# A graph layer's keys: products two tiles ahead, squares one tile ahead, and a count two steps later

## Chip, cores and metric

One core of a Trainium2 chip. The metric is the device time of one execution in microseconds (us). Engines are named as in the profile: PE (TensorE matmuls), PEld (its weight loads), DVE (VectorE), ACT (ScalarE), POOL (GpSimd), SP (SyncE).

## The reference, cut

There are 12500 nodes of 256 channels and 200000 edges, sorted by target. All is 32-bit.

```
xn = layernorm(x)                                   # no gain, no bias
gnn = relu(segment_sum((xn @ W)[src] * edge_weight, dst))
k, v = layernorm of each head of xn @ wk.T, xn @ wv.T   # 4 heads of 64, gain and bias
kv  = einsum('shd,she->hde', k, v) / 12500
mix = (q . kv, heads joined) @ wo.T + bo            # q = xn @ wq.T
x   = x + gnn + mix
h   = layernorm(x) * ln_w + ln_b
30 times: h = h + 0.01 tanh(h);  h = h sigmoid(h);  h = layernorm(h) @ W2 + b
out = x + h
```

## The kernel before, in words

The nodes are 98 tiles of 128 rows (TensorE's partitions), in 25 groups of four. The kernel runs in three parts.

**Part one, the norm (lines 580 to 619).** Step g = 0 to 26 loads a group of x, takes its statistics, shifts and scales it on ACT (line 521), transposes it (PE line 533 into a PSUM pool called p_t, copied by ACT line 539 to `xnT`, in the profile `big`), and works off the lists of edges. From g = 3 each step also takes one tile of *keys*, a class `KeyValue`: two matrix products, four matmul records, into a tile `pkv` of the PSUM pool p_kv, which has three buffers (line 290); the Square of it on ACT (line 297); the sums of squares per head on DVE (line 301); the square root on ACT (line 303); and, in `normed`, the reciprocal (line 307) and the product of `pkv` with it, `kn` (line 308), which is the last reader of the PSUM tile. There are three `kn` tiles, used in turn; the small tiles of this chain are in a pool of two buffers each. `kv_product(t)` sums the outer products of keys and values over all tiles in one PSUM tile `pacc` (PE line 316); it is called for the tile two before. So 24 tiles of keys are done in part one.

In step g = 22 (`NL` is 21) the function `any_outside` counts, on DVE, the edges whose target lies outside a fixed window of nodes; a matmul with a column of ones sums the count over partitions (line 557), and DVE turns it into a flag (line 558). After the loop all engines read the flag (line 621) and branch on it (line 626). The branch holds a slow way of summing edges; with these inputs it isn't entered, and the trace has no row of its lines.

**Part two, the loop over the remaining keys (lines 824 to 843).** It goes over tiles t = 24 to 97 and two steps more. Between the keys it sums edges. An indirect DMA on POOL (line 187, "gather") fetches the rows of `xn` of 128 edges to an SBUF tile `xg`, of which there are 16; eight gathers are an *octet*. `selections` builds on DVE the matrices that place the edges (lines 213, 218, 226: five operations for an octet). `sum_quad`, called twice for an octet, multiplies eight gathered tiles with them on PE (line 239, 16 records into `pq`); `copy_quads` copies `pq` on ACT in the step after (line 250); `add_quads` adds it to the ring of nodes `pa` on PE (line 261); `free_nodes` takes finished nodes from the ring (ACT line 275, DVE memset line 276). An octet's work is done in the steps that a small planner marks in `octet_at` (lines 802 to 808): t = 30, 33, 37, 41, 44, 48, 51, 55, 58, 62, 65, 69, 72, 76, 79, 83, 86 and 98. Two octets' gathers are issued ahead of the loop (line 809, `gathers(ROWS)`); the others follow the octet that frees their tiles, on POOL behind that octet's `pq`.

Within a step each engine has its instructions in the order of the code, for instance PE: product of t, `pacc` of t - 2, `pa`, `pq`. ACT: copy of `pq`, copy of the ring, Square of t, root of t. DVE: memset of the ring, sum of t, selections, small weights' work on some steps (`rest`), reciprocal and `kn` of t.

**Part three (from about 400 us to the end).** 30 rounds of the second network over all tiles, with the rest of the edges between them, in an order planned ahead on the host. It also uses p_kv in its first steps (lines 858 on).

Of the kernel before, what the change touches and what calls it, by code (L numbers as in the profile page):

```python
# [8 lines left out]
F32 = mybir.dt.float32  # L9
# [7 lines left out]
P = 128  # L17
# [14 lines left out]
def gps_layer(  # L32
# [22 lines left out]
    nc = tc.nc  # L55
    N, C = x.shape
# [3 lines left out]
    NT = -(-N // P)  # L60
# [7 lines left out]
    p_t = ctx.enter_context(tc.tile_pool(name="p_t", bufs=2, space=PSUM))  # L68
# [253 lines left out]
    kv_done = 0  # L322
    with ExitStack() as ph:
# [159 lines left out]
        nc.vector.tensor_scalar(w0p, tcol, jt, float(STEP // O), ALU.subtract, ALU.mult)  # L483
        nc.vector.tensor_scalar(w0p, w0p, float(OFF), 0.0, ALU.add, ALU.max)
        nc.vector.tensor_scalar(w0p, w0p, float(NT * P - WIN2), None, ALU.min)
        dfirst, dmin, dmax = (prep.tile([P, NCH], F32, name=n) for n in ("dfirst", "dmin", "dmax"))
        nc.vector.memset(dfirst, 0.0)
        nc.vector.memset(dmin, 1e9)
# [52 lines left out]
        def any_outside():  # L541

            lo = small.tile([P, NCH], F32, name="lo")
            nc.vector.tensor_tensor(lo, dfirst, w0p, ALU.max)
            hi = small.tile([P, NCH], F32, name="hi")
            nc.vector.tensor_scalar(w0p, w0p, float(WIN2), None, ALU.add)
            nc.vector.scalar_tensor_tensor(hi, dfirst, float(WIN), w0p, op0=ALU.add, op1=ALU.min)
            nc.vector.tensor_tensor(lo, dmin, lo, ALU.is_lt)
            nc.vector.tensor_tensor(hi, dmax, hi, ALU.is_ge)
            nc.vector.tensor_tensor(lo, lo, hi, ALU.add)  # L550
            cnt1 = small.tile([P, 1], F32, name="cnt1")
            nc.vector.tensor_reduce(cnt1, lo, AX.X, ALU.add)
            ones = prep.tile([P, 1], F32, name="ones")
            nc.vector.memset(ones, 1.0)
            flag_i = prep.tile([1, 1], I32, name="flag_i")
            pcnt = p_t.tile([1, 1], F32, name="pt")
            nc.tensor.matmul(pcnt, lhsT=cnt1, rhs=ones, start=True, stop=True)
            nc.vector.tensor_scalar(flag_i, pcnt, 1.0, None, ALU.min)
            return flag_i
# [20 lines left out]
        for g in range(NG + 2):  # L580
            if g + 2 < NG:
                load_x(g + 2)
            if g + 2 < NL:
                load_list(g + 2)
            if g >= 2:
                norm_of_x(g - 2)
            if 1 <= g <= NG:
                shift_of_x(g - 1)
            if g < NL:
                list_values(g)  # L590
            if 0 < g < NG:
                stats_of_x(g)
            if g == 1:
                nc.vector.tensor_reduce(hm, wh, AX.X, ALU.add)
                nc.vector.tensor_scalar(hm, hm, 1.0 / D, None, ALU.mult)
                nc.vector.tensor_tensor(wh, wh, hm[:, :, None].to_broadcast([P, KC * 2 * HEADS, D]), ALU.subtract)
            if 0 <= g - 2 < NL:
                list_stored(g - 2)
            kv = None
            if g >= 3:  # L600
                kv = KeyValue(kv_done)
                kv_done += 1
                kv.squares()
            if g >= 2:
                transposes_of_x(g - 2)
                copy_of_x(g - 2, 0)
            if kv:
                kv.deviations()
            if g >= 2:
                copy_of_x(g - 2, 1)  # L610
            if kv_done >= 3:
                kv_product(kv_done - 3)
            if 0 <= g - 1 < NL:
                list_extremes(g - 1)
                list_transposes(g - 1)
            if kv:
                kv.normed()
            if g == NL + 1:
                flag_i = any_outside()

        n_out = nc.values_load(flag_i[0:1, 0:1], min_val=0, max_val=1)


# [2 lines left out]
    with tc.If(n_out > 0):  # L626
        with ExitStack() as pg_:
# [12 lines left out]
            for t in range(NE):  # L640
                rows = P if t < EC else ER
                xg = gp.tile([P, C], F32, name="xg")
                nc.gpsimd.indirect_dma_start(
                    out=xg[:rows], out_offset=None, in_=xnd,
                    in_offset=bass.IndirectOffsetOnAxis(ap=src_i[:rows, t : t + 1], axis=0),
                )
                d_i = gp.tile([P, 1], I32, name="d_i")
                nc.sync.dma_start(out=d_i[:rows], in_=dst[t * P : t * P + rows].rearrange("(p o) -> p o", o=1))
                d = gp.tile([P, 1], F32, name="d")
                nc.vector.tensor_copy(d[:rows], d_i[:rows])  # L650
                d = d[:rows]

                w0 = float(win(t // O))
                o1 = gp.tile([P, 1], F32, name="o1")
                o2 = gp.tile([P, 1], F32, name="o2")
                ewl = gp.tile([P, 1], F32, name="ewl")
                r1 = rel[:rows, t : t + 1]
                nc.vector.tensor_scalar(o1[:rows], r1, 0.0, None, ALU.is_lt)
                nc.vector.scalar_tensor_tensor(
                    o2[:rows], r1, float(WIN) - 0.5, o1[:rows], op0=ALU.is_gt, op1=ALU.add  # L660
                )
                nc.vector.scalar_tensor_tensor(o1[:rows], d, w0 - 0.5, o2[:rows], op0=ALU.is_lt, op1=ALU.add)
                nc.vector.scalar_tensor_tensor(
                    o2[:rows], d, w0 + float(WIN2) - 0.5, o1[:rows], op0=ALU.is_gt, op1=ALU.add
                )
                nc.vector.scalar_tensor_tensor(
                    ewl[:rows], o2[:rows], 0.5, ew[:rows, t : t + 1], op0=ALU.is_gt, op1=ALU.mult
                )
                pb = p_t.tile([P, P], F32, name="pt")
                nc.tensor.transpose(pb[:, :rows], d.to_broadcast([rows, P]), ident[:rows, :rows])  # L670
                junk = gp.tile([P, P], F32, name="junk")
                cnt = gp.tile([P, 1], F32, name="cnt")
                nc.vector.scalar_tensor_tensor(
                    junk[:rows, :rows], pb[:rows, :rows], d, below[:rows, :rows], op0=ALU.is_equal,
                    op1=ALU.mult, accum_out=cnt[:rows],
                )
                sel = gp.tile([P, P], F32, name="sel")
                nc.vector.tensor_scalar(
                    sel[:rows, :rows], pb[:rows, :rows], d, ewl[:rows], ALU.is_equal, ALU.mult
                )  # L680

                move = gp.tile([P, 1], F32, name="move")
                nc.vector.tensor_sub(move[:rows], rowno[:rows], d)
                nc.vector.scalar_tensor_tensor(
                    move[:rows], cnt[:rows], 0.5, move[:rows], op0=ALU.is_gt, op1=ALU.mult
                )
                idx = gp.tile([P, 1], I32, name="idx")
                nc.vector.tensor_tensor(idx[:rows], move[:rows], d, ALU.add)
                pg = p_kv.tile([P, C], F32, name="pkv")
                nc.tensor.matmul(pg[:rows], lhsT=sel[:rows, :rows], rhs=xg[:rows], start=True, stop=True)  # L690
                ms = gp.tile([P, C], F32, name="ms")
                nc.scalar.copy(ms[:rows], pg[:rows])
                nc.gpsimd.indirect_dma_start(
                    out=acc, out_offset=bass.IndirectOffsetOnAxis(ap=idx[:rows, 0:1], axis=0),
                    in_=ms[:rows], in_offset=None, compute_op=ALU.add,
                )
            nc.sync.dma_start(out=wg, in_=gnn_weight.rearrange("(k p) c -> p k c", p=P))
            for gi, (t0, nt) in enumerate(groups):
                ac = gp.tile([P, G, C], F32, name="ac", bufs=1)
                load_rows(acc, ac, t0, nt, nc.sync)  # L700
                for j in range(nt):
                    pt = p_t.tile([P, KC, P], F32, name="pt")
                    for k in range(KC):
                        nc.tensor.transpose(pt[:, k, :], ac[:, j, k * P : (k + 1) * P], ident)
                    aT = gp.tile([P, KC, P], F32, name="aT")
                    nc.scalar.copy(aT, pt)
                    pg = p_kv.tile([P, C], F32, name="pkv")
                    for k in range(KC):
                        nc.tensor.matmul(
                            pg, lhsT=aT[:, k, :], rhs=wg[:, k, :], start=(k == 0), stop=(k == KC - 1)  # L710
                        )
                    nc.vector.tensor_copy(ac[:, j, :], pg)
# [4 lines left out]
    with ExitStack() as ph:  # L717
# [106 lines left out]
        for t in range(kv_done, NT + 2):  # L824
            copy_quads()
            free_nodes()
            kv = None
            if t < NT:
                kv = KeyValue(t)
                kv.squares()  # L830
                kv.deviations()
            if octet_at[t]:
                selections(2)
            if t in rest:
# [404 lines left out]
```

## Time and profile before

| | us |
|---|---|
| runs | 4182.11, 4190.81, 4192.11 |
| median | 4190.81 |
| profiled execution, its own time | 4187.49 |
| its span | 4185.7 |
| PE busy, share of the span | 4057.6, 97% |
| DVE, ACT, POOL busy | 3401.4, 2523.0, 2577.9 |
| mean granted clock of PE | 0.991 |

How to read the lines. In the page's group lines stand the line, engine, operation, tile written <- tiles read with shape, and count; then the total busy time and the mean of one in ns; then the idle time just before them and what ended most of it. In a timeline: start in us, duration, engine, line, operation, and in brackets the idle time before and its releaser. In the view of waits: who waited <- for whom, then the total in us, the number of waits and the longest. PE's matmuls are pipelined: the end of a record overlaps the next, so four records of a keys' product are 1.93 us long but 1.77 us apart from the next product's start. The chain of work that ended last gives line 290 3% of the span, against 53% for the product of the 30 rounds on line 1070.

### The profile page before, as it was taken

How to read it: one execution, taken by the hardware profiler on the slowest of the kernel's cores; microseconds unless marked ns; L12 is line 12 of the kernel's file. 1: busy time of each engine (PE TensorE's matmuls, PEld its weight loads, DVE VectorE, ACT ScalarE, POOL GpSimd, SP SyncE). 2: the span in 40 equal slices, each digit the busy share in tenths (PEclk: the TensorE clock that was granted, in tenths of full speed). 3: DMA queues.
4: the chain of work that ended last, by engine and by line, in shares of the span. 5: the costliest groups of instructions: out<-in, count | busy, mean ns of one | idle time of the engine just before them, and what ended most of it. 6: DMA issues, size and time to landing. Idle time of an engine off the chain costs nothing.

```text
span 4185.7 us, 67249 instructions
## 1 busy us (share of the span) xinstructions
PE 4057.6 (97%) x23817; PEld 3358.3 (80%) x23817; DVE 3401.4 (81%) x7400; ACT 2523.0 (60%) x3762; POOL 2577.9 (62%) x3189
## 2 busy tenths in 40 slices
PE   8897899999999999999999999999999999999999
PEld 5444678888888888888888888888888888888888
DVE  8554568888888888888888888888888888888887
ACT  7331246666666666666666666666656666667775
POOL 3564666777777777777777777777667652222222
PEclk9898999999999999999999999999999999999999
DMA  8332532222222222222222222222222210000000
GB/s 262 108 87 72 147 98 66 65 61 65 75 61 72 76 64 74 73 66 71 72 65 72 77 65 72 70 74 61 72 70 59 65 50 14 6 6 1 1 1 23
DMA packets 147685, 278.31 MB, mean 66 GB/s; under 512 B 28048, under 2 KB 97198, under 8 KB 147342
## 3 DMA queue, kind: packets, MB, share of 16 engines
q0 software_dynamic: 75024, 204.97, 17.0%
q1 hardware_dynamic: 72173, 68.42, 5.4%
q8 instruction: 194, 3.18, 0.3%
q14 instruction: 150, 1.22, 0.1%
q10 hardware_dynamic: 144, 0.52, 0.0%
HBM read 247.68 MB, written 26.12 MB: 65 GB/s over the span
## 4 chain that ended last, share of the span: by engine, by line
PE 77%; DVE 11%; ACT 3%; issue 3%; POOL 2%; another core or an unknown queue 1%; POOLq 0%; DVEq 0%; ACTq 0%
PE po L1070 53%; PE pt L1057 13%; PE pq L239 4%; DVE z L1043 4%; PE pkv L290 3%; PE pa L261 3%; DVE st L1029 2%; DVE s L1022 2%; ACT s L1016 2%; POOL rs L1035 1%; PE pacc L316 1%; ACT s L1023 1%; POOL xg L187 0%; DVE big L1129 0%
## 5 line engine op out<-in xcount | busy, mean ns | idle before, releaser
L1070 PE MATMUL po<-w,zT 128*128 128x256 f32 x11760 | 2669.8, 380 | 4.8 <-ACT zT L1064 2.3
L1070 PEld LDWEIGHTS po<-w,zT 128*128 128x128 f32 x11760 | 2178.4, 190 | 285.2 <-issue 7.8
L187 POOL DMA_INDIRECT xg<-xnd,src_i x1563 | 1597.4, 1022 | 512.9 <-issue 308.6
L1023 ACT ACTIVATE s<-s 128x1024 f32<-128x1024 f32 (+1 forms) x750 | 780.5, 1041 | 598.5 <-DVE s L1022 584.9
L1043 DVE TENSOR_SCALAR z<-s,st,rs 128x256 f32<-128x256 f32 x2940 | 1031.5, 418 | 100.7 <-POOL rs L1035 96.0
L1029 DVE BATCH_NORM_STATS2 st<-s 128x6 f32<-128x512 f32 x1470 | 938.7, 680 | 181.6 <-ACT s L1023 163.8
L1022 DVE SCALAR_TENSOR_TENSOR s<-s,po 128x1024 f32<-128x1024 f32 x725 | 864.3, 1192 | 251.4 <-ACT s L1016 181.3
L1016 ACT ACTIVATE s<-po 128x1024 f32<-128x1024 f32 x725 | 729.6, 1006 | 209.0 <-PE po L1070 197.6
L1064 ACT ACTIVATE zT<-pt 128x512 f32<-128x512 f32 x1470 | 801.5, 602 | 61.2 <-PE pt L1057 55.0
L1057 PE MATMUL pt<-ident,z 128*128 128x128 f32 x5880 | 792.7, 276 | 38.9 <-DVE z L1043 37.5
L1057 PEld LDWEIGHTS pt<-ident,z 128*128 128x128 f32 x5880 | 670.1, 141 | 182.6 <-issue 81.6
L1035 POOL TENSOR_TENSOR rs<-ve,mhalf 128x4 f32<-128x4 f32 (+1 forms) x750 | 763.3, 1018 | 62.5
L1033 POOL TENSOR_SCALAR ve<-st 128x4 f32<-128x4 f32 (+1 forms) x750 | 147.3, 196 | 933.6 <-DVE st L1029 889.0
L250 ACT COPY sq<-pq 128x256 f32<-128x256 f32 x196 | 72.4, 369 | 284.3 <-PE pq L239 198.2
L239 PE MATMUL pq<-xg,sel 128*32 128x256 f32 x3126 | 222.9, 386 | 8.5 <-issue 6.4
L290 PE MATMUL pkv<-wkv,big 128*128 128x512 f32 x392 | 201.3, 634 | 9.3 <-DVEq L626 4.9
L239 PEld LDWEIGHTS pq<-xg,sel 128*32 128x32 f32 x3126 | 84.7, 109 | 112.1 <-issue 69.5
L261 PE MATMUL pa<-selq,sq 128*128 128x192 f32 (+1 forms) x784 | 163.4, 331 | 9.3 <-ACT sq L250 3.6
L275 ACT COPY aT<-pa 128x128 f32<-128x128 f32 x196 | 51.4, 262 | 194.1 <-PE pa L261 145.6
L261 PEld LDWEIGHTS pa<-selq,sq 128*128 128x128 f32 (+1 forms) x784 | 137.9, 192 | 22.0 <-ACT sq L250 4.7
L301 DVE TENSOR_REDUCE v<-sq 128x8 f32<-128x512 f32 x98 | 66.7, 680 | 92.4 <-ACT sq L297 78.4
L297 ACT ACTIVATE sq<-pkv 128x512 f32<-128x512 f32 x98 | 57.9, 591 | 115.3 <-PE pkv L290 69.1
(163 smaller groups left out, 1553.2 us busy)
## 6 DMA issues: line engine op xcount, KB each, us to landing
xg<-xnd,src_i POOLq DMA_INDIRECT x1563
xt<-in_x_dram SPq DMA_DIRECT2D x48, 512.0 KB
xnd<-xt SPq DMA_DIRECT2D x24, 512.0 KB
out_dram<-big SPq DMA_DIRECT2D x24, 512.0 KB
xt<-accw SPq DMA_DIRECT2D x22, 512.0 KB
ac<-accw SPq DMA_DIRECT2D x2, 512.0 KB
xg<-in_dst_dram SPq DMA_DIRECT2D x6, 128.0 KB
xg<-in_src_dram SPq DMA_DIRECT2D x6, 128.0 KB
```

The source lines that it names most:

```text
L187: nc.gpsimd.indirect_dma_start(out=ed.xg[t], out_offset=None, in_=xnd, in_offset=bass.IndirectOffsetOnAxis(ap=src_i[:, t : t + 1], axis=0),)
L239: nc.tensor.matmul(ed.pq[j * 2 * WIN : (j + 1) * 2 * WIN, :], lhsT=sel[:, j, :], rhs=ed.xg.pop(q * Q + j), start=(q % 2 == 0), stop=last, ...
L261: nc.tensor.matmul(pa[:, k, :], lhsT=sq[:rows, k * P : (k + 1) * P], rhs=selq[:rows, :], start=False, stop=(o == NO - 1), skip_group_check ...
L1016: nc.scalar.activation(flat(s, nt), flat(h, nt), AF.Tanh)
L1022: nc.vector.scalar_tensor_tensor(sf, sf, 0.01, flat(h, nt), op0=ALU.mult, op1=ALU.add)
L1023: nc.scalar.activation(sf, sf, AF.Silu)
L1029: nc.vector.bn_stats(st[:, q, :], s[:, q].rearrange("p c j -> p (c j)"))
L1035: nc.gpsimd.tensor_tensor(rs[:, :nt], ve[:, :nt], mhalf[:, :nt], ALU.pow)
L1043: nc.vector.tensor_scalar(z[:, j, :], s[:, j // 2, :, j % 2], sv[:, j, 1:2], rs[:, j : j + 1], ALU.subtract, ALU.mult)
L1057: nc.tensor.transpose(pt[:, i, k, :], z[:, 2 * q + i, k * P : (k + 1) * P], ident)
L1064: nc.scalar.activation(zT[:, 2 * q : 2 * q + 2], pt, AF.Copy, bias=1.0)
L1070: nc.tensor.matmul(po[:, j // 2, :, j % 2] if paired else po[:, j, :], lhsT=lhsT(j, k), rhs=rhs[:, k, :], start=(k == 0 and (j % 2 == 0 or ...
```

## The change

There are four edits.

1. `any_outside` returns its count; a new function `outside_flag` holds the matmul with the ones and the flag, and is called two steps later (g = 24). The ones are set earlier, on POOL.
2. The products of the next two tiles, 24 and 25, are issued ahead of the read of the flag, in a dictionary `kvs`.
3. In step t of the loop the product of tile t + 2 is issued first, then Square, sums and root of t + 1 (in the first step of t and t + 1), then selections and the rest as before, then reciprocal and `kn` of tile t. `kv_product(t - 2)` stays where it was.
4. In the branch that isn't entered two PSUM tiles come from p_t instead of p_kv, since two tiles of p_kv are held across it.

No buffer is added: p_kv has three, the small pool two, and there are three `kn`.

```diff
+        ones = prep.tile([P, 1], F32, name="ones")
+        nc.gpsimd.memset(ones, 1.0)
...
             cnt1 = small.tile([P, 1], F32, name="cnt1")
             nc.vector.tensor_reduce(cnt1, lo, AX.X, ALU.add)
-            ones = prep.tile([P, 1], F32, name="ones")
-            nc.vector.memset(ones, 1.0)
+            return cnt1
+
+        def outside_flag(cnt1):
             flag_i = prep.tile([1, 1], I32, name="flag_i")
             pcnt = p_t.tile([1, 1], F32, name="pt")
             nc.tensor.matmul(pcnt, lhsT=cnt1, rhs=ones, start=True, stop=True)
...
             if g == NL + 1:
-                flag_i = any_outside()
-
+                cnt1 = any_outside()
+            if g == NL + 3:
+                flag_i = outside_flag(cnt1)
+
+
+        kvs = {t: KeyValue(t) for t in (kv_done, kv_done + 1)}
         n_out = nc.values_load(flag_i[0:1, 0:1], min_val=0, max_val=1)
...
-                pg = p_kv.tile([P, C], F32, name="pkv")
+                pg = p_t.tile([P, C], F32, name="pt")
...
         for t in range(kv_done, NT + 2):
             copy_quads()
             free_nodes()
-            kv = None
-            if t < NT:
-                kv = KeyValue(t)
-                kv.squares()
-                kv.deviations()
+            if t + 2 < NT:
+                kvs[t + 2] = KeyValue(t + 2)
+
+            for u in (t, t + 1) if t == kv_done else (t + 1,):
+                if u in kvs:
+                    kvs[u].squares()
+                    kvs[u].deviations()
+            kv = kvs.pop(t, None)
             if octet_at[t]:
                 selections(2)
             if t in rest:
                 rest[t]()
             if kv:
                 kv.normed()
             kv_product(t - 2)
             add_quads()
```

More of the change, by code (lines that the diff above doesn't have):

```diff
@@ L706, in gps_layer @@
                     nc.scalar.copy(aT, pt)
-                    pg = p_kv.tile([P, C], F32, name="pkv")
+                    pg = p_t.tile([P, C], F32, name="pt")
                     for k in range(KC):
```

## The prediction, made before the changed kernel ran

> **What bounds the kernel now.** I read four views, in this order: the page with its slices, the windows by stage, the waits of the keys' middle, and timelines of it. The slices say that the first tenth is the only part where PE is not full:
>
> ```profile
> PE   8897899999999999999999999999999999999999
> ...
> L290 PE MATMUL pkv<-wkv,big 128*128 128x512 f32 x392 | 201.3, 634 | 9.3 <-DVEq L626 4.9
> L301 DVE TENSOR_REDUCE v<-sq 128x8 f32<-128x512 f32 x98 | 66.7, 680 | 92.4 <-ACT sq L297 78.4
> L297 ACT ACTIVATE sq<-pkv 128x512 f32<-128x512 f32 x98 | 57.9, 591 | 115.3 <-PE pkv L290 69.1
> ```
>
> See that the product of keys is one tile in 4 records, and that its squares and their sums (ACT, DVE) spend 115 and 92 us idle, most of it for the step before them in the chain product, Square, sum. The windows by stage (length; busy us and count of PE, PEld, DVE, ACT, POOL; granted clock; DMA share; GB/s):
>
> ```profile
> 102.00:125.00 23.00, 15.95 (x78) 9.50 (x78) 10.92 (x38) 14.12 (x30) 2.09 (x4) 0.82 0.28 93
> 125.00:155.00 30.00, 22.00 (x96) 11.01 (x100) 13.15 (x32) 5.76 (x13) 17.00 (x19) 0.73 0.50 155
> 155.00:347.00 192.00, 175.82 (x1014) 93.15 (x1007) 107.49 (x275) 56.06 (x144) 122.45 (x128) 0.98 0.31 88
> ...
> 400.00:4185.00 3785.00, 3724.11 (x21967) 3172.83 (x21966) 3156.48 (x6650) 2355.39 (x3377) 2372.51 (x2920) 1.00 0.20 59
> ```
>
> The diff touches nothing after 400 us; that stage follows the keys whole, so I carry it over unchanged. What can move is 102 to 400 us. In the keys' middle PE has 175.8 us of records in 192, yet it doesn't set the pace. Line 187 on POOL starts a batch of 8 gathers every 11.9 us (179.04, 190.93, 202.84, 214.85, 226.82): 8 x 1.25 us of issue, then a wait of 2.1 to 2.3 us. The waits of that window (total, times, longest) and the timeline of ACT and POOL say what it is:
>
> ```profile
> ACT sq L297 <- PE pq L239: 40.6, 12, 4.1
> POOL xg L187 <- PE pq L239: 34.1, 13, 8.1
> ...
> PEld pacc L316 <- DVE kn L308: 6.8, 9, 1.1
> ```
>
> ```profile
> 190.49 0.60 ACT L297 ACTIVATE sq<-pkv 128x512 f32<-128x512 f32 x1 [4.02 <-PE pq L239]
> 191.84 0.30 ACT L303 ACTIVATE sd<-v,eps_t 128x8 f32<-128x8 f32 x1 [0.75 <-DVE v L301]
> 192.05 0.58 ACT L297 ACTIVATE sq<-pkv 128x512 f32<-128x512 f32 x1
> ```
>
> ```profile
> 190.93 0.95 POOL L187 DMA_INDIRECT xg<-xnd,src_i  x1 [2.19 <-PE pq L239]
> ```
>
> The product behind the first Square ended at 186.24, and the second's at 188.48, but the Squares start together, from 190.49; in quiet steps a Square starts some 0.1 us after its product. So in the second half of a batch PE's signals come late, and come in one burst, about 1.7 us after the last gather (188.74), and POOL's next batch goes on the same burst. I read that as the loop: batch 10 us, burst 1.7, signal 0.2. PE has reached the edges' product pq (line 239) before that: about 0.5 us early where octets are four steps apart, 1.7 where three.
>
> **Part 1: the count two steps later.** In the step g=22 PE waits for the count on DVE, ahead of the keys' product:
>
> ```profile
> 104.16 0.19 PE L557 MATMUL pt<-ones,cnt 128*1 128x1 f32 x2 [2.88 <-DVE ones L554]
> 104.28 3.78 PE L290 MATMUL pkv<-wkv,big 128*128 128x512 f32 x4
> ```
>
> The Square behind it starts at 108.15, after 3.85 us of idle ACT, and ACT is otherwise continuous there. With the matmul two steps later the Square finds its product ready: I take -3.5, as DVE's seven small operations of the count still stand in the step; bounds -3.9 (the whole idle) and -2.5 (some 1 us of DVE's queue comes through). The later flag needs one column of PE and one DVE operation (0.1 and 0.2 us), with its input two steps old: 0. The memset moved to POOL runs early: 0.
>
> **Part 2: two products ahead of the branch.** PE ends its last work before the branch at 120.30, DVE its last kn at 121.90, and PE resumes at 125.17. Two products take 2 x 1.77 = 3.6 us of issue, 120.2 to 123.8. They fit in the 4.9 us that PE spends waiting; the flag is DVE's, ahead of them, so the branch isn't later: 0. If PE's queue delays PE's own branch, the bound is +1. After it the first product took 3.75 us against 1.94 warm:
>
> ```profile
> 125.17 3.75 PE L290 MATMUL pkv<-wkv,big 128*128 128x512 f32 x4 [4.87 <-DVEq L626]
> ```
>
> Here the page "TensorE: Matmul & The Clock Gate" of the Trainium skill, in Part 1, gives an activity window of about 3.4 us at half clock. By it, an idle under 3.4 us would cost no cold product; the row at 104.28 has 3.78 us after 2.88 us of idle, so the measurement decides against counting on it.
>
> The two tiles' squares, 2 x 0.6, then go at once when ACT is back. The gain at the first step is up to 3.75 us of product; but the stage to 155 us is bound by the 16 gathers (POOL 127.11 to 147.14) and the held Squares of the tiles behind them (139.45 and 150.10). There the first pq, at 153.91, stands behind pacc of 152.84, which waited 3.95 us for kn. In the new order two more products and one more set of squares, sums and kn stand ahead of that pq. One such chain, Square to kn, is 2.7 us (190.49 to 193.17); of the products one is already done. I take +2.9 (2.7 plus a signal), bounds 0 (the burst at 150 lets it through) and +7.5 (that and a cold product of 3.75 and a pacc of 1.1).
>
> **Part 3: the loop's order.** Nothing is added: the same 4 records, one Square, sum, root, reciprocal and kn per tile. What moves is who waits. The PSUM pool of the keys has three tiles, and the product of t+2 now takes the tile of t-1, which kn of t-1 must have left; that is the last DVE operation of the step before. On DVE kn(t) now stands behind the sum of t+1, and in an octet's step behind five selections (193.69 to 194.94, 1.25 us). In a quiet step the loop is product 1.93, signal 0.1, Square 0.6, sum 0.69, root 0.30, reciprocal 0.20, kn 0.69, and signals of some 0.1 each between them, 4.35 us or a little more, for two steps of 2.24 = 4.48. So a quiet step stays at 2.24, with 0.13 us to spare, where before a tile had a whole step.
>
> An octet's step has no such room. pq(t) is now behind the product of t+2, and so behind kn of t-1, whose Square is among the signals that are held. After the burst PE before went on at once (pkv at 191.02, 0.5 us after 190.49). Now it waits for Square 0.6, sum 0.69, selections 1.25, reciprocal and kn 1.0: 3.7 us with the signals. Its work of the step follows: product 1.77, pacc 0.5, pa 0.7. The second step behind the burst so begins 6.67 us after it instead of 4.76 (195.17 less 190.41): +1.9. A signal held in the step ahead of pq costs 0.8 (PE's nine waits for kn, 6.8 us) to 1.3 us (the longest that PE's own queue shows there), say 1.0, as PE now hangs on it. From these 2.9 the slack goes. The octets' steps (30, 33, 37, 41, 44, and so on to 83) lie seven times three apart and eight times four: 7 x (2.9 - 1.7) + 8 x (2.9 - 0.5) = +27.6. Bounds: 0, if the wait is no longer than the slack, and 15 x 3.2 = +48 (1.9 + 1.3, nothing covered). Below nothing is the second rival.
>
> The page "Perfetto Trace Analysis" of the Trainium skill, section "Optimization Strategy", says that the same gap repeated on the engine that should be full can mean that PSUM has no room for the next tile. In the trace of before the repeated gap is the gathers' signal, not room; this change would be the one to make the rule true, since two tiles ahead need a fourth buffer to be free of kn.
>
> **Part 4: the tail.** The last two steps issue no product, and the tail's waits from 382.9 to 398 are for the last gathers: PE has 4.01 us of records in those 18. I take -1, bounds -3 and +2. The pool of the branch's own tiles is in code that isn't entered: 0.
>
> **Sum.** -3.5 + 0 + 2.9 + 27.6 - 1 = +26.0 on the profiled execution of 4187.49 us (span 4185.7, so 1.8 around it): 4213.5. The median of the runs is 3.3 higher, within their spread of 10; I leave it out and say 4213.
>
> **Rivals.**
> *A batch-bound middle.* The batches keep 11.9 us, as pq still runs ahead of the burst. For it: the slack, and 2.24 us of PE against 11.9 / 3.5 = 3.4 us a step. Against it: PE's 92%. Then -3.5 + 2.9 - 1 = -1.6: 4186, the same.
> *Faster, on the other side.* Products two ahead put pq and the Squares in the first half of a batch, before signals are held; then POOL needn't wait for the burst, and batches go at 10.0 us (8 x 1.25). It decides if pq's signal reaches POOL before its eighth gather ends. Price: 15 x 1.9 = -28.5, with -1.6: 4157. Against it: pq needs PE's records of the steps before, some 10 us of the 10, and the quiet loop has 0.13 us of room.
> *It isn't two ahead.* With three PSUM tiles the third product always waits for kn, so the lead is one tile in every octet and PE stands still on DVE in quiet steps too. If the loop is 4.8 instead of 4.35 us, 55 quiet steps lose 0.16 each (4.8 / 2 less 2.24), some 9 us on top of the forecast: 4222.
>
> **How the numbers follow.** Forecast with its bounds 0.54, the third rival 0.06, batch-bound 0.28, faster 0.12. A measurement of this kernel can tell about 0.3%, 12.6 us, from no change. Of the forecast 0.09 lies under +12.6, the rest is slower: 0.45, and 0.06 of the third. Batch-bound gives 0.25 the same, 0.03 slower by its startup bound (+7.5, with octets of +0.4). Faster: 0.10, and 0.02 of it within. So faster 0.10, same 0.36, slower 0.54. The range goes from the batch-bound case with its best bounds (4187.5 - 3.9 - 3 = 4181) to the forecast with every upper bound (4187.5 - 2.5 + 7.5 + 48 + 2 = 4242). Left out are the faster case, 0.12, and some 0.05 of mishaps on top of each other.
>
> **What would show it.** Right: at 104 us no gap ahead of the keys' product; products ahead of the branch after 120 us; in the middle, waits of PE's weight loads for DVE's kn at the products (line of pkv), which the trace of before doesn't have, and batches 13 to 14.5 us apart. Batch-bound: 11.9 us, POOL's wait for pq near 2.2 us. Faster: batches of 10 to 11 us, and POOL's wait for pq gone. The forecast is wrong if PE's late signals are no property of the batches but of the order in which PE issues.

## The result, and the profile after

| | before | after |
|---|---|---|
| median of 7 runs, us | 4189.1 | 4200.57 |
| lowest and highest | 4182.11 to 4193.27 | 4196.66 to 4206.58 |
| profiled execution, its own time | 4187.49 | 4206.58 |
| its span | 4185.7 | 4204.7 |

The change makes the kernel slower, by a ratio of 1.003 (95% interval 1.0019 to 1.0042), 11.5 us between the medians. The profiled execution of after is the slowest of its seven: its +19.0 us of span is more than the median shows, so the sums below explain that one execution.

The page after, the slices and the groups. PE's product of keys (line 290) used to have 9.3 us of idle time in front of it; now it has 52.4, and DVE's kn ends 43.2 of them. The sums' idle time on DVE went from 92.4 to 67.9, with no gain in time:

```profile
PE   8787899999999999999999999999999999999999
...
L290 PE MATMUL pkv<-wkv,big 128*128 128x512 f32 x392 | 204.7, 648 | 52.4 <-DVE kn L308 43.2
...
L301 DVE TENSOR_REDUCE v<-sq 128x8 f32<-128x512 f32 x98 | 67.1, 685 | 67.9 <-ACT sq L297 52.6
```

The windows by stage, the same four as before. In 102 to 125 PE has 19 records more, those of the two products ahead of the branch and of the first product and `pacc` behind it. In the keys' middle it has 158.6 us of records in 192 where it had 175.8. After 400 us nothing differs but the shift: from the keys' last `pacc` to the end of the span the kernels need 3805.2 and 3806.6 us:

```profile
102.00:125.00 23.00, 19.82 (x97) 10.02 (x95) 12.65 (x44) 14.42 (x31) 4.86 (x8) 1.00 0.37 118
125.00:155.00 30.00, 17.55 (x62) 9.29 (x63) 11.42 (x27) 6.05 (x14) 14.24 (x15) 0.66 0.44 136
155.00:347.00 192.00, 158.57 (x916) 85.90 (x915) 96.30 (x250) 51.71 (x130) 106.63 (x113) 0.95 0.27 77
...
400.00:4185.00 3785.00, 3715.28 (x21930) 3167.69 (x21931) 3153.46 (x6643) 2353.33 (x3374) 2384.81 (x2932) 0.99 0.20 59
```

Where the 19.0 us came from, by the starts of POOL's gathers in both traces (a batch is the eight gathers behind an octet's pq):

| point | before | after | shift | gained in this stretch |
|---|---|---|---|---|
| first gather | 127.11 | 123.55 | -3.6 | -3.6 |
| batch 1 | 155.24 | 157.55 | +2.3 | +5.9 |
| batch 16 | 335.54 | 358.26 | +22.7 | +20.4 |
| batch 18 | 379.11 | 397.31 | +18.2 | -4.5 |
| span's end | 4185.7 | 4204.7 | +19.0 | +0.8 |

The 15 distances from batch 1 to 16 were 11.8 to 13.4 us, mean 12.02. They are now of two kinds: 11.9 to 12.0 (eight), and 13.4 to 16.5 (seven); mean 13.38. The planner's steps tell which: the seven distances between octets three steps apart grew by 0.25 us in all, the eight between octets four steps apart by 20.2 us, the first six by 1.4 to 4.5 us each and the last two by less than 0.1.

One of the long ones (184.24 to 200.57), in the timelines of PE, ACT and DVE after. The gathers are issued until 193.92:

```profile
190.14 1.96 PE L290 MATMUL pkv<-wkv,big 128*128 128x512 f32 x4
191.93 0.63 PE L316 MATMUL pacc<-kn 128*65 128x65 f32 x8
195.78 2.65 PE L290 MATMUL pkv<-wkv,big 128*128 128x512 f32 x4 [3.21 <-DVE kn L308]
198.23 1.08 PE L316 MATMUL pacc<-kn 128*65 128x65 f32 x8
199.24 1.60 PE L239 MATMUL pq<-xg,sel 128*32 128x256 f32 x16
```

```profile
195.84 0.60 ACT L297 ACTIVATE sq<-pkv 128x512 f32<-128x512 f32 x1 [4.11 <-remote]
```

```profile
191.31 0.19 DVE L307 RECIPROCAL rs<-sd 128x8 f32<-128x8 f32 x1
195.03 0.69 DVE L308 TENSOR_TENSOR kn<-pkv,rs 128x512 f32<-128x512 f32 x1 [3.53 <-remote]
```

Read it backwards. pq came at 199.24, 5.3 us behind the gathers' end, where before it came with that end (188.88 against 188.74). It stood behind the product of 195.78, which waited 3.21 us for kn. That kn had its reciprocal at 191.5 and the PSUM tile long since; what it still needed is its own tile, which `pacc` of three tiles before had to have left. That matmul's record ended at 190.2, and kn went on at 195.0, 1.1 us after the last gather. The Square that waits for the product ended at 192.1 went on at 195.84. ("remote" is how the view names a release that it can't tie to an instruction; that it was `pacc`'s is worked out from what kn needs.) After its idle time PE's product took 2.65 us instead of 1.96. In the next octet, three steps on, the kn that waits (2.84 us, to 212.06) is one that comes behind pq (209.16), and the batch comes after 11.9 us.

### The profile page after: what moved, and what is told of

It reads as the page before. It is cut to its first block, busy times and chain, and to the rows that moved or that the text cites. A ratio compares the mean times of both kernels' runs of the same rounds, so it can differ in the third digit from the quotient of the medians.

```text
span 4204.7 us, 67211 instructions
## 1 busy us (share of the span) xinstructions
PE 4055.9 (96%) x23817; PEld 3360.4 (80%) x23817; DVE 3400.8 (81%) x7399; ACT 2524.4 (60%) x3762; POOL 2576.7 (61%) x3190
## 4 chain that ended last, share of the span: by engine, by line
PE 74%; DVE 13%; issue 3%; ACT 3%; POOL 2%; another core or an unknown queue 1%; DMA 0%; POOLq 0%; DVEq 0%; ACTq 0%
PE po L1080 51%; PE pt L1067 13%; PE pq L239 4%; DVE z L1053 4%; DVE st L1039 3%; PE pa L261 3%; PE pkv L290 3%; DVE s L1032 2%; ACT s L1026 1%; POOL rs L1045 1%; POOL xg L187 1%; PE pacc L316 1%; ACT s L1033 1%; DVE kn L308 0%
## 5 line engine op out<-in xcount | busy, mean ns | idle before, releaser
L1043 POOL TENSOR_SCALAR ve<-st 128x4 f32<-128x4 f32 (+1 forms) x750 | 147.1, 196 | 934.3 <-DVE st L1039 890.5
L290 PE MATMUL pkv<-wkv,big 128*128 128x512 f32 x392 | 204.7, 648 | 52.4 <-DVE kn L308 43.2
L290 PEld LDWEIGHTS pkv<-wkv,big 128*128 128x128 f32 x392 | 71.2, 200 | 117.4 <-issue 67.9
L301 DVE TENSOR_REDUCE v<-sq 128x8 f32<-128x512 f32 x98 | 67.1, 685 | 67.9 <-ACT sq L297 52.6
```

## The experiments

Three theories were named as the runs went on. Theory 1, **room**: with three PSUM tiles the product of t+2 waits for kn of t-1, and pq stands behind it. Theory 2, **order**: the sums of t+1 stand ahead of kn of t on DVE. Theory 3 takes both links together, and theory 4 adds kn's own tiles. Ratios are to the kernel before on the same chip.

**The count alone.** Edit 1 of the change, in the kernel before.

> Only the count's matmul is moved two steps later; branch and key loop as before. Every theory: the keys' product of step g=22 no longer waits for the count, the branch comes 3.5 us earlier, the gathers too, and the middle keeps its 12.0 us from batch to batch: 3 to 4 us less than before, ratio 0.9991.

Measured: 4186.8 us, ratio 0.9987 (0.9978 to 0.9996). The first gather is at 123.83, 3.3 us earlier, as expected, and the interval holds the 3 to 4 us. The middle did not keep its pace everywhere: the second batch followed the first directly (151.8, 162.3), and the third came 19.2 us later. ACT's timeline shows why: while the second batch was issued the copy of pq waited 8.4 us, and the next Square then 4.6.

```profile
161.03 0.30 ACT L303 ACTIVATE sd<-v,eps_t 128x8 f32<-128x8 f32 x1 [0.76 <-DVE v L301]
169.74 0.37 ACT L250 COPY sq<-pq 128x256 f32<-128x256 f32 x1 [8.40 <-remote]
174.70 0.60 ACT L297 ACTIVATE sq<-pkv 128x512 f32<-128x512 f32 x1 [4.59 <-PE pkv L290]
```

The pq in question was issued at 159.99 and its records are 1.07 us long.

**One tile ahead.**

```diff
-        kvs = {t: KeyValue(t) for t in (kv_done, kv_done + 1)}
+        kvs = {t: KeyValue(t) for t in (kv_done,)}
-            if t + 2 < NT:
-                kvs[t + 2] = KeyValue(t + 2)
+            if t + 1 < NT:
+                kvs[t + 1] = KeyValue(t + 1)
```

> The changed kernel with products one tile ahead instead of two (one product ahead of the branch), squares and sums still one tile ahead. Theory 1 (room: the product of t+2 waits for kn of t-1, which is held with PE's late signals, and the edges' pq stands behind it): the product now needs kn of t-2, so the wait goes, batches come back to 12.0 us apart, time 4 us below before to 2 above. Theory 2 (order: the sums of t+1 and the selections stand ahead of kn of t on DVE): nothing changes against the changed kernel, 10 to 14 us above before.

Measured: 4196.92, ratio 1.0007 (0.9997 to 1.0016), between the two theories' numbers. Most distances are back at 11.7 to 11.9, but two, of 18.8 and 18.0 us, bring the mean to 12.72.

**Products two ahead, the step's own Square.**

```diff
-            for u in (t, t + 1) if t == kv_done else (t + 1,):
-                if u in kvs:
-                    kvs[u].squares()
-                    kvs[u].deviations()
             kv = kvs.pop(t, None)
+            if kv:
+                kv.squares()
+                kv.deviations()
```

> The changed kernel with products two tiles ahead, but Square, sums and root of tile t in step t, as before. Theory 1: the product of t+2 still waits for kn of t-1, 8 to 14 us above before. Theory 2: kn of t has nothing new ahead of it, so 4 us below before to 2 above.

Measured: 4188.08, ratio 0.9986 (0.9976 to 0.9996): theory 1 by itself falls, and theory 2's number holds. The waits from 155 to 340 us show that the room is as short as in the changed kernel, and that the batches don't notice it here:

```profile
PE pkv L290 <- DVE kn L308: 17.9, 18, 2.6
DVE kn L308 <- PE pq L239: 9.4, 6, 2.1
DVE kn L308 <- PE pacc L316: 4.4, 4, 1.6
DVE kn L308 <- remote: 4.1, 4, 1.3
```

PE waits for kn 18 times, 17.9 us, but pq still comes ahead of the late signals, and the batches are 12.20 apart. Kn's own waits for PE are shorter (the last three rows: 17.9 us, longest 2.1) than in the changed kernel (28.7 us, longest 3.5). The start does show the room: the first batch is at 157.15, as late as in the changed kernel, against 151.8 with the count alone.

**The product last in the step**, behind pq: the two lines of `kvs[t + 2]` move to the end of the loop's body.

> The changed kernel with the product of t+2 issued as the last of step t, behind pq, instead of the first; the rest the same. Theory 1: pq no longer stands behind the wait for kn, batches 12.0 us apart, 4 us below before to 2 above. Theory 2: as the changed kernel, 10 to 14 us above before.

Measured: 4193.27, ratio 1.0005 (0.9996 to 1.0014), 1.3 us between the medians, within theory 1's range; mean distance 12.44, with one of 19.2. It is 6.5 us above the count alone; whether the early squares or the product's place cost that, this run doesn't separate.

**Five PSUM tiles**, the order untouched:

```diff
-            self.pkv = p_kv.tile([P, 2 * HEADS, D], F32, name="pkv")
+            if t >= 26 and (t - 24) % 5 >= 3:
+                self.pkv = p_t.tile([P, 2 * HEADS, D], F32, name="pt")
+            else:
+                self.pkv = p_kv.tile([P, 2 * HEADS, D], F32, name="pkv")
```

> The changed kernel with five PSUM tiles for the keys in the loop (the three, and two of the pool that the transposes used), the order untouched: the product of t+2 then needs kn of t-3. Theory 3 (both links together: kn of t stands on DVE behind the sum of t+1, which waits for the late signal of the product of t+1, and the product of t+3, with pq behind it, waits for that kn): the loss in the middle goes, batches 11.8 to 12.3 us apart against 13.4, time 5 us below before to 2 above. Theory 2 (order alone): as the changed kernel, 8 to 14 us above before.

Measured: 4181.1 against 4187.03, ratio 0.9983 (0.9974 to 0.9992): 5.9 us below, 0.9 past theory 3's range and far from theory 2's. Room was needed for the loss. The same view and window of the changed kernel, and then of this one (whose lines are three further down):

```profile
POOL xg L187 <- PE pq L239: 54.4, 10, 14.0
PEld pkv L290 <- DVE kn L308: 29.5, 17, 3.5
...
PE pkv L290 <- DVE kn L308: 23.8, 15, 3.2
DVE kn L308 <- remote: 15.5, 5, 3.5
DVE kn L308 <- PE pacc L316: 8.7, 3, 3.0
DVE kn L308 <- PE pq L239: 4.5, 2, 2.8
```

```profile
POOL xg L187 <- PE pq L239: 32.8, 13, 7.4
...
DVE kn L311 <- PE pq L239: 14.5, 5, 3.5
DVE kn L311 <- PE pacc L319: 8.6, 4, 3.0
DVE kn L311 <- remote: 4.7, 2, 2.4
```

kn waits for PE as long as it did (27.8 us by these three rows, 28.7 by the last three above). But no product waits for kn any more: the line is gone, for this tile and for its other pool's. The first batch is at 150.0 instead of 157.55, so the start's loss was room too. The distances are 11.8 to 12.0 but for 14.3 and one of 18.2, mean 12.51, above the 11.8 to 12.3 expected. The ACT row of the longest is this:

```profile
317.16 0.37 ACT L250 COPY sq<-pq 128x256 f32<-128x256 f32 x1 [13.78 <-remote]
```

**kn first**: reciprocal and kn of t stand ahead of Square and sums of t+1 in the step, three PSUM tiles.

> The changed kernel with reciprocal and kn of tile t ahead of Square and sums of t+1 in the step (and so ahead of the selections), the rest the same, three PSUM tiles. Theory 3: the other link is broken, batches 11.8 to 12.3 us apart, time 7 to 1 us below before. Theory 1 (room alone): PE's wait for kn of t-1 is the same as in the changed kernel, 8 to 14 us above before.

Measured: 4197.69 against 4187.03, ratio 1.0025 (1.0015 to 1.0035), theory 1's number. Taking the sums of t+1 from ahead of kn doesn't remove the loss, so that order on DVE, as theory 3 had it, is not the link. kn, now at the head of DVE's queue, itself waits for PE, and longer than in the runs above (the three rows make 50.3 us):

```profile
DVE kn L308 <- PE pq L239: 20.7, 7, 4.7
PE pkv L290 <- DVE kn L308: 18.8, 12, 3.2
DVE kn L308 <- remote: 18.8, 7, 4.8
DVE kn L308 <- PE pacc L316: 10.8, 5, 2.6
```

The end of the keys' last `pacc` in the profiled executions puts these kernels in nearly the same order: five PSUM tiles 374.0, the count alone 377.5, before 380.5, own squares 380.6, product last 382.1, one ahead 385.3, kn first 392.2, after 398.1. What follows it, 3805.0 to 3811.4 us, differs by up to 6.4 us between executions of code that the change doesn't touch.

**No gathers**, in the kernel before and after. Both leave out the fetches of octets 3 to 18 and read the first two octets' rows again, so part of the edges' sums is of other rows.

> The kernel before without the gathers of octets 3 to 18: it reads the rows of the first two octets again, so that part of the edges' sums is of other rows. Theories 1 to 3 take PE's late signals for the gathers' doing: without gathers no Square waits over 1.5 us, and the distance of two pq is PE's own work, about 10 us against 12.0. If the late signals come from PE's order itself, the waits of 4 us stay.

> The changed kernel without the gathers of octets 3 to 18, as in the run beside it. Theory 3: the new order costs only where signals are late, so its pq lie within 0.3 us of those of the kernel before without gathers, about 10 us apart. If the quiet loop itself is too long (product, Square, sum, kn in two steps), they are 11 us apart or more and PE waits for kn in most steps.

Measured in one run each: 4145.98 and 4155.4, so the order costs 9.4 us with nothing to make PE's signals late. From pq 1 to pq 16 the two need 148.3 and 155.3 us, 9.88 and 10.35 an octet: 0.47 more, beyond the 0.3 allowed, so it isn't only the late signals. It falls on every octet: in the quiet part octets three and four steps apart are 8.52 and 10.76 us apart before, 9.02 and 11.26 after. From the first gather to pq 1 the start grew by 7.2 us, from 26.6 to 33.8. The waits of 4 us are gone while no gathers are issued: from 155 to 310 us none of ACT for PE's products is over 2.3 us in the kernel before (1.5 was expected). They come back with the gathers: eight are issued from 311.24 to 320.96, and in that kernel the Square of a product that ended at 318.47 then starts at

```profile
322.80 0.60 ACT L305 ACTIVATE sq<-pkv 128x512 f32<-128x512 f32 x1 [4.06 <-remote]
```

After, there is a short wait at each octet; the timeline of PE, lines eight further down:

```profile
193.69 1.98 PE L298 MATMUL pkv<-wkv,big 128*128 128x512 f32 x4 [0.51 <-DVE kn L316]
...
205.50 1.96 PE L298 MATMUL pkv<-wkv,big 128*128 128x512 f32 x4 [0.84 <-DVE kn L316]
```

**The last four kernels** shared a chip on which the kernel before took 4087.03 us (25 runs, 4085.38 to 4089.73). Its traces show no late signals in the keys' middle, although the gathers are whole in three of them: in the one of these with three PSUM tiles the Squares' longest wait for a product is 1.3 us, in place of 4 and more. There is no trace of the kernel before on it.

*Four kn tiles*: the changed kernel with `kns[t % 4]` in the loop.

> The changed kernel with four kn tiles in the loop instead of three (the fourth in the place of a small tile that shares another's now), three PSUM tiles. Theory 4: what holds kn, and by it the product two tiles on, is the late signal of pacc of t-3, the last reader of kn's tile; with four it is pacc of t-4, a step older: batches 12.0 to 12.6 us apart, time 4 us below before to 3 above. Theory 3 with the PSUM tiles alone (the late Square in front of kn on DVE): kn waits as long as now, 8 to 14 us above before.

Measured: 4097.39 against 4087.03, ratio 1.0024 (1.0014 to 1.0034). Since no signal was late, it can't decide theory 4. It tells something else: the loss is there without late signals, as in the pair without gathers, and isn't kn's tiles then. Its batches are 10.38 apart, its pq 10.36, as in the changed kernel without gathers (10.35). PE's timeline, and the DVE rows that lead to its wait:

```profile
191.18 1.88 PE L290 MATMUL pkv<-wkv,big 128*128 128x512 f32 x4
192.90 0.63 PE L316 MATMUL pacc<-kn 128*65 128x65 f32 x8
194.51 1.96 PE L290 MATMUL pkv<-wkv,big 128*128 128x512 f32 x4 [0.97 <-DVE kn L308]
```

```profile
191.75 0.17 DVE L276 MEMSET pa<- 128x128 f32 x1 [0.85 <-ACT aT L275]
192.18 0.69 DVE L301 TENSOR_REDUCE v<-sq 128x8 f32<-128x512 f32 x1 [0.27 <-ACT sq L297]
192.78 0.75 DVE L798 TENSOR_SCALAR ws<-ws,wm 128x256 f32<-128x256 f32 x2
193.45 0.18 DVE L307 RECIPROCAL rs<-sd 128x8 f32<-128x8 f32 x1
193.67 0.69 DVE L308 TENSOR_TENSOR kn<-pkv,rs 128x512 f32<-128x512 f32 x1
```

In the step behind an octet PE's `pa` (to 191.35) releases ACT's copy of the ring, then come Square, sum, the weights' work of that step, and kn, all in one file; the next product waits for that kn.

*Five PSUM tiles and four kn.*

> The changed kernel with five PSUM tiles and four kn tiles. If kn's wait for pacc still counts beside the five PSUM tiles: 3 us or more below the run with five PSUM tiles, 10 to 15 below before. If the PSUM tiles were the whole of it: as that run, 4 to 10 us below before.

Measured: 4082.85, ratio 0.9989 (0.998 to 0.9998). Batches 10.05 and pq 9.81 apart, and no product waits for kn. It is not below the run with five PSUM tiles alone (0.9983), so the fourth kn shows no gain.

*Five PSUM tiles, the step's own Square.*

> Products two tiles ahead, Square and sums of the step's own tile, five PSUM tiles, three kn. If squares a tile ahead are worth nothing by themselves, the time is that of the changed kernel with five PSUM tiles, 4 to 10 us below before. If they are what brings that kernel below before, this one is as the one with three PSUM tiles and the step's own squares, 6 below before, or less.

Measured: 4080.59, ratio 0.9985 (0.9976 to 0.9994), pq 9.85 apart, the same as with early squares within the intervals. Those show no gain by themselves. On this chip three PSUM tiles cost about as much in the start as in the octets: the first pq is at 146.1 with three and four kn, at 138.5 and 139.4 with five, and from pq 1 to pq 16 it is 155.5 us against 147.7 and 147.1.

*Thin gathers.* The changed kernel, in which the gathers of octets 3 to 18 fetch 16 of 128 rows.

> The changed kernel, but the gathers of octets 3 to 18 fetch 16 of their 128 rows (the other rows are those of an octet before, so part of the edges' sums is of other rows): as many gathers and the same work on POOL, an eighth of the data. If PE's signals are late because the gathers' data are on their way, they are on time: no wait of ACT for PE over 2.7 us in the middle, batches as far apart as PE's pq without gathers, 10.4 us, or by POOL, 11 at most. If POOL's issuing is what delays them, batches stay 13 us or more apart.

Measured in one run: 4100.61, pq 10.36 us apart. Whole gathers and four kn tiles give 10.36 on that chip too, so it tells nothing on whether data or issuing makes the signals late. With its three kn tiles it does show no gain of a fourth where signals are on time.

## Why the prediction was right, and where it was not

**The sign and the range.** Forecast slower, 4213 in 4181 to 4242; measured 4200.57. The sum was +26.0, the medians moved by 11.5 and the profiled pair by 19.0. The sign rests on the octets' term, which was right in size where octets are four steps apart and wrong where they are three apart; part of the nearness is luck, as the errors of the other terms go both ways.

**The count: -3.5.** The first gather moved by -3.6 after, and by -3.3 with the count alone. Right.

**The branch: 0.** The two products stand at 116.80 in eight records, ahead of the branch. The first product behind it took 1.95 us with no idle time shown, not 3.75. This saved product went into the start, which was late anyway.

**The start: +2.9.** From first gather to first batch the stretch grew by 5.9 us, inside the bounds of 0 and 7.5. The term was too small. The one chain that was counted, Square to kn, was right in kind; but PE met it twice, once with 6.86 us of idle time ahead of a product at 129.88 and once with 7.56 at 147.12, both ended by kn, both followed by a cold product (one after idle time) of 3.75 and 3.78. The first kn stood behind the preparation of the lists and the first selections on DVE (122.81 to 126.77), the second waited 7.65 us, until 2.8 us after the last of the 16 gathers. With five PSUM tiles the first batch is at 150.0, so this was room.

**The octets: +27.6, 1.84 each.** Measured +20.4, 1.36 each, in the profiled execution. The mechanism holds: product behind kn, pq behind the product, the batch behind pq. That needs the room, as five PSUM tiles show. The step that failed is which signal is late: the prediction had kn of t-1 wait for a held Square, with the sums and selections ahead of it. The rows show kn with its reciprocal done, waiting for a signal of PE, by what it needs `pacc`'s, and with kn ahead of the sums on DVE the loss stays. That it is the three kn tiles is only argued; the run meant to show it met a chip without late signals. Nor is it shown what the early squares add. They are needed for the loss, since the run with own squares differs from the changed kernel in nothing else, has the same three PSUM and three kn tiles, and loses nothing; the waits of kn are shorter there. The size failed by kind of octet. Of the +27.6, the seven octets three apart were to give 8.4 and gave 0.25, as the kn that waits stands behind pq there; the eight that are four apart were to give 19.2 and gave 20.2, which is close in part by luck, since single ones range from less than 0.1 to 4.5.

**The quiet loop's 0.13 us to spare.** The sum doesn't come out as written: the terms listed make 4.51 us before the further signals, over the 4.48 of two steps. The root's 0.30 us doesn't belong in it, since kn takes a root made a step earlier (in the stretch taken apart above the root is at 186.19, the reciprocal at 189.08); without it the terms make 4.21. The conclusion held: without gathers PE's waits for kn are at the octets, and a step more between two octets is still 2.24 us (11.26 less 9.02). The third rival's loop of 4.8 us is refuted. But the octet's own serial chain, 0.47 us, is there with signals on time. There the change costs 9.4 us: 7.0 in the 15 octets and 7.2 in the start, less 3.5 by the count and 1.3 behind pq 16.

**The tail: -1.** Measured -4.5, but the loop of before with the count moved shows -4.0 in the same stretch (336.5 to 376.1, against 335.54 to 379.11). It is not the new order's.

**The batch-bound rival** (4186) describes the run with products two ahead and own squares: PE waits, the batches don't notice. **The faster rival** can't have its price with late signals: batches did go nearly end to end, 10.5 to 11.0 us apart, in three kernels, and the next distance was 18.8 to 19.2; in the one taken apart PE's signal to ACT then stayed late into the second batch.

**Room.** The page "Perfetto Trace Analysis" of the Trainium skill, section "Optimization Strategy", says that a repeated gap on the engine that should be full can mean that PSUM has no room for the next tile. The changed kernel agrees: 15 waits of PE for kn, 23.8 us, and none with two tiles more. The run with own squares qualifies it: 18 such waits in the middle, and no time lost by the median.

**What stays open:** which of PE's signals holds kn where they are late, whether a fourth kn would help there, and why own squares avoid the loss with three PSUM tiles; and how much of the median's 11.5 us is octets, since it was one profiled execution, slower than the median, that was taken apart.

## What to carry to other kernels

Issuing a product two tiles ahead with three buffers doesn't put it two ahead of its reader: count the buffers from the last reader in program order, and look at what else stands behind the blocked instruction; here it was the edges' product that starts the next eight gathers. Five tiles, with two that lay idle in another pool, turned +0.30% into -0.17% (0.9983, 0.9974 to 0.9992; each against the kernel before on its own chip), and by the intervals no version with room differs from moving the count alone (0.9987). An earlier start need not carry through the stage: with the count alone the first gather was 3.3 us earlier, batch 16 was 1.0 later, and the keys ended 3.1 earlier, in one execution.

## What the runs showed of the hardware

In the traced runs with gathers but the last four, PE's signals to other engines came late while gathers were being issued back to back. In the changed kernel's batch of 184.24 the last Square on time is at 190.08, 5.8 us in, and kn went on 1.1 us after the last gather; in the kernel before the Squares went on 1.75 us after it (190.49 against 188.74), and behind the 16 gathers of the start 2.8 us (after) and 3.0 us (before) passed. The end of the gathers is not always what lets the signals come: with the count alone the copy of pq went on at 169.74, with gathers issued until 172.1. The longest wait is the copy's 13.78 us with five PSUM tiles. Its pq had ended at 305.35, it started at 317.16, and between 298.57 and 316.05 there were 14 gathers with no gap above 0.45 us. What links gathers and signals is not shown, only that the waits go and return with the gathers in the run without octets 3 to 18.

On the chip of the last four the same gathers had no such effect, batches went at 10.0 us (eight times 1.25) with room, and the kernel before was 100 us shorter, 4087.03 against 4187.03. What makes the difference wasn't found. The ratio of the changed order was nearly the same on both (1.003, and 1.0024 with a fourth kn), though on that chip three PSUM tiles cost about as much in the start as in the octets.
